# Cross attention taken by two pairs of heads a step, with part of the score copies on ScalarE

## The chip, the cores and the metric

The kernel runs on one core of one Trainium2 chip. A core has TensorE (PE, the matrix engine; PEld is its loading of the stationary operand), VectorE (DVE), ScalarE (ACT), GpSimd (POOL) and SyncE (SP), which here only issues transfers. Matrix products are written to PSUM, of which this kernel uses eight banks of 128x512 float32 values (two pools, of seven and of one), and read from there by VectorE or ScalarE; everything else on the chip lies in SBUF, and the DMA queues move data between SBUF and memory (HBM, "dram" tiles in the code). The metric is the device time of one execution in microseconds (us), lower is better, as the median of several runs. An error bound on the output has to be kept, and float32 products have to stay float32.

## The reference, cut to what matters

One block of a perceiver: eight batches (B) of 128 rows (S) with 512 features (D) attend to 2048 context rows (J) of 384 features, then to themselves, then pass a feed-forward layer. LayerNorm without parameters stands ahead of each of the three.

```python
def cross(x, context, Wq, Wk, Wv, Wo, bo):          # x is already normalized
    q = (x @ Wq).reshape(B, 128, 8, 64)              # 8 heads of 64
    k = (context @ Wk).reshape(B, 2048, 8, 64)
    v = (context @ Wv).reshape(B, 2048, 8, 64)
    sim = jnp.einsum('bihd,bjhd->bhij', q, k) * 64 ** -0.5
    attn = jax.nn.softmax(sim, axis=-1)
    out = jnp.einsum('bhij,bjhd->bihd', attn, v).reshape(B, 128, 512)
    return out @ Wo + bo

def self_attention(m, Wq, bq, Wk, bk, Wv, bv):       # m is normalized
    logits = (m @ Wq + bq) @ (m @ Wk + bk).T         # a batch at a time
    logits = where(causal, -inf, logits)
    probs = softmax(logits, axis=1) / sqrt(512)      # over the queries
    return m + probs @ (m @ Wv + bv)

def ffn(x, w1, b1, w2, b2):                          # h and w2 in an 8-bit float
    h = relu(x @ w1.T + b1)
    return fq16(fq8(h) @ fq8(w2).T + fq16(b2))

x = x + cross(layernorm(x), context, ...)
x = x + self_attention(layernorm(x), ...)
x = x + ffn(layernorm(x), ...)
```

## The kernel before

**Cross attention, batch by batch.** The main loop (L925 to L1005) goes over eight batches b and, in each, over four pairs of heads m. Of a pair, `scores` (L499) makes 128x2048 scores of each of two heads: for each of four stretches of 512 keys it fills two banks, one per head, by matmuls on 64 rows of the array each (a head has 64 features, so two heads stand above one another: tile 64*128 in the profile). VectorE moves each bank into the tile `p` and takes its maximum along the way (L515); L521 and L523 make the negated, scaled maximum `nm` of the pair from the eight partial ones. `exps` (L532) is one ScalarE instruction per head over 2048 keys, with the row sums as a by-product. `turns` (L540) turns `p` in 32x32 blocks by eight VectorE transposes, four per head (L548), and 16 DMAs issued by SyncE put the blocks into `pT` (L554), which has the keys on partitions. `attend` (L559) multiplies `pT` by v into the accumulating bank `po`; each head fills 64 columns of the array (tile 128*64).

`after_strips` (L526) is a one-element ScalarE copy that reads a partial maximum, set between a pair's scores and the transfers that ScalarE issues next.

**Keys and values as units.** K and V of a batch come out of four units: `k_proj` for each half of the heads (kt0, kt1) and `v_proj` for each half of the context rows (v0, v1). A unit is a `block_product` (L300): a fast matrix multiplication in which sums of blocks of the operands (`x_both` and `m_both`, made by GpSimd in `next_half`, L828; `wk_sums` and `wv_sums`) are multiplied in 20 products instead of more, and the results are combined while leaving PSUM. It uses seven banks, and into several of them later products are added after an earlier state has been read:

```python
mm(z3, 7, True)
mm(z3, 8, False)
take((2, 0), z3)
yield
mm(z1, 12, True)
mm(z2, 19, True)
take((1, 0), z2)
mm(z3, 2, False)
```

`take` is a ScalarE copy from a bank into the result (L328), `with_bank` and `less_bank` are VectorE additions and subtractions with a bank (L331, L334). The three `yield`s divide a unit into parts of 2, 5, 4 and 9 products; `first_of(unit)` writes the next part, `all_of(unit)` the rest. Later in the unit the fourth product on z4 follows `with_bank((3, 1), z4, add, (3, 1))`, and the second on z2 follows `take((1, 0), z2)`, as above. A K product is two matmuls of 512 columns (of 256 in the first batch's `k_proj(0, 1, (1,))`, which makes only half of the keys), a V product four of 256 columns.

In a step (b, m) the order is: scores of pair m, products with v of the pair before, first exponential, the unit's first part, second exponential, transposes and strips, the rest of the unit. The units of a batch make the keys and values of the next; in the first batch `k_proj(0, 1, (1,))` and `v_proj(0, 1)` stand in m = 0, and `both_weights` (L289) between them. `project` (L673) multiplies the result of a batch by wo (held in SBUF all along) in the first step of the next and adds it to the rows x; `norm_rows` (L650) and others then make the normalized, turned rows for self attention, spread over the steps m = 1 to 3, and ScalarE's queue writes them out.

**Ahead of and behind the loop.** `turn_weight` (L275) turns the two weights of self attention by VectorE transposes and 16 SyncE issues each (L284) into `turned_w`; `both_weights` multiplies the two with one another (tile `pw`, 32 matmuls) and writes the result to memory. Self attention (class `SelfAttention`, two groups sa0 and sa1 of four batches) fills steps of the last batch and follows it, then comes the feed-forward layer.

**What sets the order.** The order of TensorE, and of VectorE and ScalarE in the loop, is that of the program text (manual schedule, with lists in which ScalarE and VectorE work). SyncE's and GpSimd's instructions are ordered by the scheduler. An engine works through its list, and an instruction in it waits for the semaphores of what it depends on. Places in SBUF come from pools by tag: a new tile of a tag waits until the last reader of the tile that had the place before is done. Here `pp` (the tile `p`) and `ptp` (`pT`) have one place each, `qtp` two, `tmp` and `xp` two each, `wop` holds wq and later wo, and `keep` holds the weights of K and V at the start and later every second v0.

Of the kernel before, what the change touches and what calls it, by code (L numbers as in the profile page):

```python
# [25 lines left out]
def tile_perceiver_block(  # L26
# [35 lines left out]
    TMPB = 2  # L62
# [7 lines left out]


# [4 lines left out]
    keep = ctx.enter_context(tc.tile_pool(name="keep", bufs=1))  # L76
# [28 lines left out]
    ktp, vp, qtp, wop = right("ktp", 1), right("vp", 1), right("qtp", 2), right("wop", 1)  # L105
    pp, ptp, tmp, xp = right("pp", 1), right("ptp", 1), right("tmp", TMPB), right("xp", 2)
# [100 lines left out]
    w_in = keep.tile([P, 2, NKC, D], F32, tag="keep", name="w_in")  # L207
# [24 lines left out]
    wq = load_w(wop, xa_wq, NK, "wq", nc.sync)  # L232
# [27 lines left out]
    def spread_biases():  # L260
        for n in range(2):
            bias_rows.append(tmp.tile([P, D], F32, tag="t", name=f"row_{n}"))
            nc.gpsimd.dma_start(bias_rows[n], across(n))
# [11 lines left out]
    def turn_weight(i):  # L275

        if i == 0:
            turned_w.append(vp.tile([P, 2, NK * NK, P], F32, tag="v0", name="turned_w"))
        for k in range(NK):
            nc.vector.transpose(w_sa[:, i, k], w_sa[:, i, k])  # L280
        t = turned_w[0][:, i]
        w = w_sa[:, i].rearrange("p k (m g j) -> p g (k m) j", m=NK, g=Q)
        for a, g in STRIPS:
            nc.sync.dma_start(t[ts(g, SQ), :, ts(a, SQ)], w[ts(a, SQ), g])  # L284
# [4 lines left out]
    def both_weights():  # L289

        tq, tk = (turned_w[0][:, i].rearrange("p (k m) c -> p k m c", m=NK) for i in range(2))
        for n in range(NK):
# [5 lines left out]
            t = xp.tile([P, D], F32, tag="x", name=f"both_{n}")  # L298
            nc.scalar.copy(t, ps)
            nc.scalar.dma_start(both_w[:, n], t)  # L300
            if n == 1:
                yield
# [123 lines left out]
    def v_proj(b, h):  # L426


        pool, tag = (keep, "keep") if h == 0 and b % 2 == 0 else (vp, f"v{h}")
        v = pool.tile([P, 4, 2, D], F32, tag=tag, name=f"v_{b}_{h}")  # L430
# [65 lines left out]
    def scores(b, m):  # L496
# [8 lines left out]
        home, tag = (ktp, "kt0") if (b, m) == (B - 1, 2) else (pp, "p")  # L505
        p = home.tile([P, Q, 2, J // Q], F32, tag=tag, name=f"p_{b}_{m}")
        for n in range(NJ):
# [6 lines left out]
            for i in range(2):  # L514
                nc.vector.tensor_scalar(  # L515
                    p[:, :, i].rearrange("p g (t i) -> p t g i", i=SQ)[:, ts(n, Q)],
                    pair[i].rearrange("p (t g i) -> p t g i", g=Q, i=SQ),
                    1.0, None, ALU.mult, ALU.max, accum_out=mx[:, i, n : n + 1],
                )
# [4 lines left out]
        ps_[b, m], nms[b, m], mxs[b, m] = p, nm, mx  # L524

    def after_strips(b, m):  # L526


        seen = small.tile([P, 1], F32, tag="seen", name=f"seen_{b}_{m}")
        nc.scalar.copy(seen, mxs[b, m][:, 0, 0:1])  # L530
# [9 lines left out]
    def turns(b, m):  # L540

        p = ps_[b, m]
        pt = ptp.tile([P, Q, 2, J // Q], F32, tag="pT", name=f"pT_{b}_{m}")
        for i in range(2):
            for _, g in STRIPS[:Q]:
                nc.vector.transpose(p[:, g, i], p[:, g, i])  # L548
        turned_[b, m] = pt.rearrange("p a h (t i) -> p h t a i", i=SQ)

        def strips(engines, some):

            for i, (a, g) in enumerate(some):
                engines[i % len(engines)].dma_start(pt[ts(g, SQ), a], p[ts(a, SQ), g])  # L554

        return strips
# [34 lines left out]
    def spread_sums(b):  # L591
        line = wides[b]
        rs = wides[b] = tmp.tile([P, D], F32, tag="t", name=f"rs_{b}")
        for i in range(2):
# [3 lines left out]
            )  # L598

    def inverse_sums(b):  # L600
# [3 lines left out]
        wide = tmp.tile([P, NH, DH], F32, tag="t", name=f"wide_{b}")  # L604
        nc.vector.tensor_copy(wide, rden.unsqueeze(2).to_broadcast([P, NH, DH]))
        wides[b] = wide.rearrange("p h d -> p (h d)")

    def normalized_first(b):
# [4 lines left out]
        rs = tmp.tile([P, D], F32, tag="t", name=f"rs_{b}")  # L613
# [14 lines left out]
    def load_x(b):  # L628
        xs[b] = xp.tile([P, D], F32, tag="x", name=f"x_{b}")
        nc.scalar.dma_start(xs[b], xd[:, b, :])  # L630

    def load_u(b):
        u = tmp.tile([P, D], F32, tag="t", name=f"u_{b}")
        nc.scalar.dma_start(u, u_line)
        stats[b] = (u,)

    def row_stats(b):
# [4 lines left out]
        stats[b] += (mv,)  # L642

    def row_scale(b):
        sd = small.tile([P, 1], F32, tag="sd", name=f"sd_s_{b}", bufs=4)
        nc.scalar.activation(sd, stats[b][1][:, 1:2], AF.Sqrt, bias=eps)
# [4 lines left out]
    def norm_rows(b):  # L651

        u, mv, sd = stats[b]
        rs = small.tile([P, 1], F32, tag="rs", name=f"rs_s_{b}", bufs=4)
        nc.vector.reciprocal(rs, sd)
        xn = tmp.tile([P, D], F32, tag="t", name=f"xn_s_{b}")
        nc.vector.tensor_scalar(xn, xs[b], mv[:, 0:1], rs, ALU.subtract, ALU.mult)
        pt = bank(f"pt_s_{b}")
        row_constant(b, xn, u, pt)
        nc.vector.tensor_tensor(xs[b], xs[b], xn, ALU.add)  # L660
        for k in range(NK):
            nc.tensor.transpose(pt[:, ts(k, P)], xn[:, ts(k, P)], ident)
        xt = tmp.tile([P, NK, S], F32, tag="t", name=f"xt_s_{b}")
        nc.scalar.copy(xt, pt.rearrange("p (k t) -> p k t", k=NK))
        stats[b] = xt
# [7 lines left out]
    def project(b, ot):  # L673
        ps = bank(f"py_{b}")
        for k in range(NK):
            nc.tensor.matmul(  # L676
                ps, ot[:, ts(k, P)], wo[:, k, :], start=(k == 0), stop=(k == NK - 1)
            )
        nc.vector.tensor_tensor(xs[b], ps, xs[b], ALU.add)

    rows = {}

    def bring_last_rows():
        rows[0] = keep.tile([P, B, D], F32, tag="keep", name="rows")
        nc.gpsimd.dma_start(rows[0][:, B - 2 :], xd[:, B - 2 :])
        for r in range(B):
            xs[r] = rows[0][:, r, :]

    def bring_rows():
        nc.scalar.dma_start(rows[0][:, : B - 2], xr[:, : B - 2])  # L690

# [11 lines left out]
    class SelfAttention:  # L703


        def __init__(self, g, pool, w):
            self.g, self.pool = g, pool
            self.both, self.swv, self.bv, self.u, self.mask = w
            self.rows = [g * GB + i for i in range(GB)]
            self.xt = pool.tile([P, NK, GT], F32, tag=f"xt{g}", name=f"xt_{g}")  # L710
            there = slice(g * GT, min((g + 1) * GT, (B - 2) * S))
# [121 lines left out]
    def enter_self_attention():  # L833
        src.close()
        wsa = ctx.enter_context(tc.tile_pool(name="wsa", bufs=1, reuse_waits="tile"))
        sap = ctx.enter_context(tc.tile_pool(name="sap", bufs=1, reuse_waits="tile"))
        both = wsa.tile([P, NK, D], F32, tag="both", name="both")
        nc.gpsimd.dma_start(both, both_w)
        w = [both, wsa.tile([P, NK, D], F32, tag="swv", name="swv")]
        sa0 = SelfAttention(0, sap, w + [None] * 3)  # L840
        nc.gpsimd.dma_start(w[1], sa_wv.rearrange("(k p) n -> p k n", p=P))
        w += [load_row(wsa, sa_bv, "bv"), load_row(wsa, u_line, "u")]
# [7 lines left out]
        w.append(mask)  # L850
        sa0.bv, sa0.u, sa0.mask = w[2:]
        return sap, w, sa0
# [22 lines left out]
    bo = tmp.tile([P, D], F32, tag="t", name="bo")  # L875
# [12 lines left out]

    wo = load_w(wop, xa_wo, NK, "wo", nc.sync, tag="wq")

# [27 lines left out]
    def turned_rows(g, rows, tag):  # L918

        xt = sap.tile([P, NK, GT], F32, tag=tag, name=f"xf_{g}")  # L920
# [4 lines left out]
    sa0 = None  # L925
    for b in range(B):
        last = b + 1 == B
        for m in range(NK):
            scores(b, m)

            if m % 2 and not last:
                after_strips(b, m)
            if m == 0 and b > 0:
                after_strips(b, m)
                spread_sums(b - 1)
            if m == 1 and b > 0 and not last:
                load_u(b - 1)
            if m == 3 and b > 0 and not last:
                nc.scalar.dma_start(xtd[:, :, ts(b - 1, S)], stats[b - 1])
                nc.scalar.dma_start(xr[:, b - 1, :], xs[b - 1])  # L940
            if m == 3 and b < B - 2:
                load_x(b)
            unit = None
            if m > 0:
                attend(b, m - 1)
            elif b > 0:

                attend(b - 1, NK - 1)
# [329 lines left out]
```

## Time and profile before

| | |
|---|---|
| median of 3 runs | 1082.82 us (1082.68 to 1082.97) |
| profiled execution, span | 1080.4 us |
| TensorE busy | 1074.7 us, 99% |
| VectorE busy | 756.8 us, 70% |
| ScalarE busy | 350.6 us, 32% |
| GpSimd busy | 249.0 us, 23% |
| granted TensorE clock | full in all 40 slices |
| moved by DMA | 136.62 MB, 126 GB/s |
| read from HBM | 55.85 MB |

The span is the time from the first to the last instruction in the one execution that was profiled; the time of a run also holds what lies around it. Busy times overlap between engines. In the chain of work that ended last, each line is a start, a duration, an engine, a tile with a line of the program, and a number of instructions. Matmul ends are modelled in the profile, and a few of their records can be missing. The costliest groups of VectorE and ScalarE, with their count, sum and mean duration of one, and the idle time ahead of them with what ended it:

```profile
L548 DVE STREAM_TRANSPOSE p<-p 128x512 f32<-128x512 f32 x256 | 158.9, 679 | 62.2 <-ACT p L535 62.0
L535 ACT ACTIVATE p<-p,nm 128x2048 f32<-128x2048 f32 x64 | 128.2, 2004 | 210.7 <-DVE nm L523 103.3
L515 DVE TENSOR_SCALAR_CACHE_REDUCE p<-sc 128x512 f32<-128x512 f32 x256 | 159.0, 686 | 20.9 <-PE sc L511 20.9
...
L328 ACT COPY v<-pv_z 128x512 f32<-128x512 f32 x112 | 62.8, 585 | 55.3 <-PE pv_z L435 55.0
```

VectorE is idle for 62 us ahead of transposes, until exponentials end, and ScalarE for 103 us ahead of exponentials, until the maxima are there; TensorE is in neither wait.

### The profile page before, as it was taken

How to read it: one execution, taken by the hardware profiler on the slowest of the kernel's cores; microseconds unless marked ns; L12 is line 12 of the kernel's file. 1: busy time of each engine (PE TensorE's matmuls, PEld its weight loads, DVE VectorE, ACT ScalarE, POOL GpSimd, SP SyncE). 2: the span in 40 equal slices, each digit the busy share in tenths (PEclk: the TensorE clock that was granted, in tenths of full speed). 3: DMA queues.
4: the chain of work that ended last, by engine and by line, in shares of the span. 5: the costliest groups of instructions: out<-in, count | busy, mean ns of one | idle time of the engine just before them, and what ended most of it. 6: DMA issues, size and time to landing. Idle time of an engine off the chain costs nothing.

```text
span 1080.4 us, 15603 instructions
## 1 busy us (share of the span) xinstructions
PE 1074.7 (99%) x5614; PEld 706.4 (65%) x5614; DVE 756.8 (70%) x1639; ACT 350.6 (32%) x559; POOL 249.0 (23%) x379
## 2 busy tenths in 40 slices
PE   9999999999999999999999999999999999999998
PEld 5485774577467657755775577557746656768875
DVE  5876567778777877787688778777877657584333
ACT  3322133324332422433243324332433222323221
POOL 0154130360055005500540262036100312000000
PEclk9999999999999999999999999999999999999999
DMA  9476334553565456535544653455345744431001
GB/s 328 139 189 152 118 78 98 146 148 84 131 166 137 93 135 164 139 86 150 152 110 99 165 147 79 117 147 147 80 111 127 235 121 147 175 106 31 10 12 58
DMA packets 74013, 136.62 MB, mean 126 GB/s; under 512 B 29376, under 2 KB 37840, under 8 KB 72912
## 3 DMA queue, kind: packets, MB, share of 16 engines
q1 hardware_dynamic: 61264, 113.03, 40.8%
q10 hardware_dynamic: 8464, 11.54, 3.6%
q0 software_dynamic: 4208, 11.06, 3.3%
q8 instruction: 45, 0.74, 0.3%
q14 instruction: 32, 0.26, 0.1%
HBM read 55.85 MB, written 10.52 MB: 61 GB/s over the span
## 4 chain that ended last, share of the span: by engine, by line
PE 98%; SPq 1%; DVE 1%; issue 0%; ACT 0%; DMA 0%; POOL 0%; POOLq 0%
PE pv_z L435 21%; PE pk_z L412 20%; PE po L566 11%; PE sc L511 10%; PE pv_b L435 4%; PE pk_b L412 3%; PE ph_b L1104 3%; PE psk L749 3%; PE psv L793 3%; PE py L676 3%; PE pq L479 3%; PE pf L1152 2%; PE ph_c L1104 2%; PE ph_a L1104 2%; PE k L395 2%; PE ph L1056 1%
## 5 line engine op out<-in xcount | busy, mean ns | idle before, releaser
L548 DVE STREAM_TRANSPOSE p<-p 128x512 f32<-128x512 f32 x256 | 158.9, 679 | 62.2 <-ACT p L535 62.0
L535 ACT ACTIVATE p<-p,nm 128x2048 f32<-128x2048 f32 x64 | 128.2, 2004 | 210.7 <-DVE nm L523 103.3
L515 DVE TENSOR_SCALAR_CACHE_REDUCE p<-sc 128x512 f32<-128x512 f32 x256 | 159.0, 686 | 20.9 <-PE sc L511 20.9
L435 PE MATMUL pv_z<-wv_sums,x_both 128*128 128x256 f32 x640 | 157.9, 381 | 0.0
L412 PE MATMUL pk_z<-x_both,wk_sums 128*128 128x512 f32 (+1 forms) x320 | 149.2, 572 | 0.7 <-ACT kt L328 0.6
L435 PEld LDWEIGHTS pv_z<-wv_sums,x_both 128*128 128x128 f32 x640 | 120.4, 190 | 18.6 <-issue 2.5
L566 PEld LDWEIGHTS po<-pT,v 128*64 128x64 f32 x2048 | 111.1, 137 | 23.8 <-issue 23.1
L566 PE MATMUL po<-pT,v 128*64 128x128 f32 x2048 | 118.8, 274 | 0.0
L511 PE MATMUL sc<-kt,q 64*128 64x512 f32 x512 | 118.5, 602 | 0.0
L435 PE MATMUL pv_z<-wv_sums,m_both 128*128 128x256 f32 x448 | 107.3, 379 | 0.0
L412 PEld LDWEIGHTS pk_z<-x_both,wk_sums 128*128 128x128 f32 x320 | 59.2, 190 | 66.9 <-issue 55.0
L412 PE MATMUL pk_z<-m_both,wk_sums 128*128 128x512 f32 (+1 forms) x224 | 101.3, 568 | 0.0
L588 POOL DMA_DIRECT2D line_s<-inverse x28 | 14.5, 525 | 350.8 <-DVE inverse L585 350.8
L435 PEld LDWEIGHTS pv_z<-wv_sums,m_both 128*128 128x128 f32 x448 | 84.2, 190 | 12.6 <-POOL x_both L165 0.6
L165 POOL TENSOR_TENSOR m_both<-x_both 128x256 f32<-128x256 f32 x70 | 51.0, 729 | 175.3 <-DMA x_both<-in_ctx_t_dram 113.9
L511 PEld LDWEIGHTS sc<-kt,q 64*128 64x128 f32 x512 | 46.9, 186 | 65.6 <-issue 54.0
L328 ACT COPY v<-pv_z 128x512 f32<-128x512 f32 x112 | 62.8, 585 | 55.3 <-PE pv_z L435 55.0
L328 ACT COPY kt<-pk_z 128x512 f32<-128x512 f32 (+1 forms) x112 | 59.7, 562 | 58.3 <-PE pk_z L412 57.9
L530 ACT COPY seen<-mx 128x1 f32<-128x1 f32 x21 | 4.0, 191 | 209.2 <-DVE p L515 209.2
L412 PEld LDWEIGHTS pk_z<-m_both,wk_sums 128*128 128x128 f32 x224 | 40.8, 190 | 46.8 <-issue 35.1
L165 POOL TENSOR_TENSOR x_both<-x_both 128x256 f32<-128x256 f32 x98 | 69.9, 727 | 3.0 <-DMA x_both<-in_ctx_t_dram 2.7
L331 DVE TENSOR_TENSOR v<-pv_z,v 128x512 f32<-128x512 f32 x96 | 63.1, 685 | 5.5 <-PE pv_z L435 5.5
(212 smaller groups left out, 1312.8 us busy)
## 6 DMA issues: line engine op xcount, KB each, us to landing
pT<-p SPq DMA_DIRECT2D x488, 128.0 KB, 2.4
x_both<-in_ctx_t_dram SPq DMA_DIRECT2D x45, 512.0 KB, 5.2
w<-in_w_t_dram SPq DMA_DIRECT2D x1, 4096.0 KB, 13.9
w2f<-in_w_t_dram SPq DMA_DIRECT2D x16, 256.0 KB, 2.7
pT<-p POOLq DMA_DIRECT2D x24, 128.0 KB, 3.9
x_in<-in_x_dram SPq DMA_DIRECT2D x8, 256.0 KB, 6.4
qd<-xq SPq DMA_DIRECT2D x8, 256.0 KB, 2.5
q<-qd SPq DMA_DIRECT2D x8, 256.0 KB, 4.1
```

Source lines behind the costliest of these rows:

```text
L165: eng.tensor_tensor(x_block(b, h, to), x_block(b, h, one), x_block(b, h, two), ALU.add if op == "+" else ALU.subtract,)
L328: nc.scalar.copy(outs[ij], views(ps))
L331: nc.vector.tensor_tensor(outs[to], views(ps), outs[other], op)
L412: nc.tensor.matmul(ps[:, : n * BK], wk_sums[:, WSLOT[WAT[r]], f2, :], x_block(b, hs, XAT[r]), start=start, stop=True, skip_group_check=True,)
L435: nc.tensor.matmul(ps[:, ts(t, 256)], x[:, ts(t, P)], wv_sums[:, WSLOT[WAT[r]], :], start=start and t == 0, stop=True, skip_group_check=True,)
L479: nc.tensor.matmul(ps, wq[:, k, ts(m, P)], xt[:, k, :], start=(k == 0), stop=(k == NK - 1),)
L511: nc.tensor.matmul(pair[i], q[r, :], kts[b, m // 2][r, m % 2, ts(n, 512)], start=True, stop=True)
L515: nc.vector.tensor_scalar(p[:, :, i].rearrange("p g (t i) -> p t g i", i=SQ)[:, ts(n, Q)], pair[i].rearrange("p (t g i) -> p t g i", g=Q, ...
L535: nc.scalar.activation(p[:, :, i], p[:, :, i], AF.Exp, bias=nms[b, m][:, i : i + 1], scale=SCALE, accum_out=sums[b][:, h : h + 1],)
L548: nc.vector.transpose(p[:, g, i], p[:, g, i])
L566: nc.tensor.matmul(pos[b][h * DH : (h + 1) * DH, ts(m, P)].rearrange("p (a i) -> p a i", a=Q), v[:, jt % 8, ts(2 * m + h, DH)], turned_[b, ...
L1104: nc.tensor.matmul(self.ps[to][:, ts(t, HR)], w[:, q, 2 * self.d + t], x[:, q], start=start and t == q == 0, stop=True, skip_group_check=True,
```

## The change

A step now takes two pairs of heads, "one" and "two": `scores` of both (sixteen banks), then `attend` of both pairs of the step before, then two units. So the loop has two halves per batch: in half 0 the two `v_proj` of the same batch (in the first batch `k_proj(0, 1, (1,))` and `v_proj(0, 1)`), in half 1 the two `k_proj` of the next batch. Three of the eight banks of each pair are copied into `p` by ScalarE, and VectorE takes their maxima from `p` afterwards, in the new function `maxima`:

```diff
+    COPIED = ((1, 0), (2, 1), (3, 0))
...
             for i in range(2):
-                nc.vector.tensor_scalar(
-                    p[:, :, i].rearrange("p g (t i) -> p t g i", i=SQ)[:, ts(n, Q)],
-                    pair[i].rearrange("p (t g i) -> p t g i", g=Q, i=SQ),
-                    1.0, None, ALU.mult, ALU.max, accum_out=mx[:, i, n : n + 1],
-                )
+                to = p[:, :, i].rearrange("p g (t i) -> p t g i", i=SQ)[:, ts(n, Q)]
+                of = pair[i].rearrange("p (t g i) -> p t g i", g=Q, i=SQ)
+                if (n, i) in COPIED:
+                    nc.scalar.copy(to, of)
+                else:
+                    nc.vector.tensor_scalar(
+                        to, of, 1.0, None, ALU.mult, ALU.max, accum_out=mx[:, i, n : n + 1]
+                    )
+        ps_[b, m], mxs[b, m] = p, mx
+
+    def maxima(b, m):
+
+        p, mx = ps_[b, m], mxs[b, m]
+        for n, i in COPIED:
+            nc.vector.tensor_reduce(
+                mx[:, i, n : n + 1], p[:, :, i, ts(n, P)], axis=AX.XY, op=ALU.max
+            )
```

`after_strips` is gone, `turns` takes one head at a time, and `strips` is a function of its own. The loop:

```diff
     for b in range(B):
         last = b + 1 == B
-        for m in range(NK):
-            scores(b, m)
...
+        for half in range(2):
+            one, two = 2 * half, 2 * half + 1
+            scores(b, one)
+            scores(b, two)
+            if half == 0 and b > 0:
+                bring_home(b - 1)
+            if half == 1 and not last:
+                load_q(b + 1)
...
+            before = (b, 0) if half else (b - 1, 2)
+            if before[0] >= 0:
+                attend(before[0], before[1])
+                attend(before[0], before[1] + 1)
+            maxima(b, one)
+            maxima(b, two)
...
+            exps(b, one, 0)
+            exps(b, one, 1)
+            turns(b, one, 0)
+            if half == 0 and b > 0:
+                ot = normalized(b - 1, wides[b - 1])
+            turns(b, one, 1)
+            strips(b, one, [nc.sync])
+            first_of(unit)
+            exps(b, two, 0)
...
+            first_of(unit)
+            turns(b, two, 0)
+            exps(b, two, 1)
+            if half == 0 and b > 0:
+                project(b - 1, ot)
+            first_of(unit)
+            turns(b, two, 1)
+            strips(b, two, [nc.sync])
+            if half == 0 and b > 0:
+                row_stats(b - 1)
+                row_scale(b - 1)
+            if half == 1:
+                sums_along_rows(b)
+            all_of(unit)
+            unit = units[1]
+            if half == 0 and b > 0:
+                norm_rows(b - 1)
+                next_half(b + 1, 0)
+                first_of(unit)
+                first_of(unit)
+                turn_rows(b - 1)
+            all_of(unit)
+            if half == 0:
+                next_half(b + 1, 1)
```

Places: `pp` and `ptp` now have two places each, `qtp` one, every v0 lies in `vp`, and `keep`, `tmp`, `xp` and `wop` are gone. What lay there at the start (w_in, wq, bias rows, `turned_w`, the copies of `pw`) lies in the places of `p` and `pT`. wo and the rows that the projection and the normalization need lie in the place of the first keys, kt0, once the scores that read those keys are done; wo (1 MB) is loaded anew for every batch, by SyncE, and three rows tiles by ScalarE's queue:

```diff
+    def bring_home(b):
+
+        home = homes[b] = ktp.tile([P, 2 * NK, D], F32, tag="kt0", name=f"home_{b}")
+        nc.sync.dma_start(home[:, :NK], xa_wo.rearrange("(k p) n -> p k n", p=P))
+        line, rs = wides[b], home[:, NK]
...
+        wides[b] = rs
+        xs[b] = home[:, NK + 1]
+        nc.scalar.dma_start(xs[b], xd[:, b, :])
+        nc.scalar.dma_start(home[:, NK + 2], u_line)
```

`norm_rows` no longer turns the rows: the sum of x and the normalized rows goes to GpSimd, and `turn_rows`, inside the second V unit, does the transposes and writes both out. `both_weights` moves from inside the first step to ahead of the first scores:

```diff
     turn_weight(1)
     all_of(values)
     next_half(1, 0)
-
-    wo = load_w(wop, xa_wo, NK, "wo", nc.sync, tag="wq")
-
+    both_weights()
```

Behind the loop the order changes. In half 1 of the last batch the first unit is the keys of sa0 (`sa0.keys`) and there is no second; the batch's logits, exponentials, two batches' values and probabilities of sa0 come ahead of the last two `attend`, which stood among them before; batch 7's rows alone (before: 6 and 7) are normalized from memory at the end; and the value weights of self attention are loaded a second time, beside w1, for the values made after the place is given up. The number of matmuls is the same.

## The prediction

> **What bounds the kernel now.** I read the page first: busy times, granted clock, shares of the chain that ended last.
>
> ```profile
> span 1080.4 us, 15603 instructions
> ...
> PE 1074.7 (99%) x5614; PEld 706.4 (65%) x5614; DVE 756.8 (70%) x1639; ACT 350.6 (32%) x559; POOL 249.0 (23%) x379
> ...
> PEclk9999999999999999999999999999999999999999
> ...
> PE 98%; SPq 1%; DVE 1%; issue 0%; ACT 0%; DMA 0%; POOL 0%; POOLq 0%
> ```
>
> TensorE is busy for all but 5.7 us, at full clock, and is 98% of the chain. So the change can only gain inside TensorE's own stream, and it loses wherever it makes TensorE wait. Next, the chain of waits for one step of an inner batch, and for one unit that follows no attention step:
>
> ```profile
> 535.69 3.43 PE py L676 x8
> 539.12 3.63 PE sc L511 x16
> 542.75 3.64 PE po L566 x64
> 546.40 6.26 PE pv_z L435 x28
> ```
> ```profile
> 66.53 6.04 PE pv_z L435 x28
> ```
>
> Scores (64x128 tiles), products with v (128x64) and projection (128x128) each stream eight times 512 columns. The projection, whose shape is its neighbours', takes 3.43; scores and products 0.20 and 0.21 more. The unit's first 28 matmuls cost 6.26 after products with v and 6.04 after another unit: 0.22. So each passage to another tile shape costs about 0.2 us. From a scores start (436.37) to the next batch's (539.12) is 102.75 us.
>
> Then the timelines of ScalarE and VectorE in one step, which give the pitch of each link that TensorE will wait for:
>
> ```profile
> 573.60 2.01 ACT L535 ACTIVATE p<-p,nm 128x2048 f32<-128x2048 f32 x1
> 575.50 0.19 ACT L535 ACTIVATION_READ_ACCUMULATOR p<-p,nm 128x1 f32 x1
> 575.59 0.57 ACT L664 COPY xt_s<-pt_s 128x512 f32<-128x512 f32 x1
> 576.06 1.57 ACT L328 COPY kt<-pk_z 128x512 f32<-128x512 f32 x3
> ```
> ```profile
> 575.72 2.49 DVE L548 STREAM_TRANSPOSE p<-p 128x512 f32<-128x512 f32 x4 [0.67 <-ACT p L535]
> 578.14 0.65 DVE L334 TENSOR_TENSOR kt<-kt,pk_z 128x512 f32<-128x512 f32 x1
> 578.79 0.69 DVE L331 TENSOR_TENSOR kt<-pk_b,kt 128x512 f32<-128x512 f32 x1
> ```
>
> Start to start: one exponential 2.0, one copy out of a bank 0.5, four transposes 2.4, one addition 0.6. In the same view eight score evacuations go every 0.61 and the negated maximum is ready 0.5 after the last.
>
> **The change, part by part.** Durations are of this execution, 1080.4 us; the median of the runs is 1082.8, so 2.4 is added at the end.
>
> *Fewer passages.* 32 groups of scores, 32 of products and as many returns to units become 16 of each. 48 passages less at 0.2 (0.18 to 0.21): **-9.3** (-8.7 to -10.1). As a check, a batch is four times 7.27 of scores and products, 80 products of units at 0.858 or 0.863, 3.43 of projection, 0.44 of transposes, four returns at 0.2: 102.6 of 102.75, so little else is there to win. The number of matmuls stays.
>
> The Trainium skill ("TensorEngine Tiling (Array Packing)", Key Properties) says that changing the tiling mode drains TensorE, which agrees with the 0.2 us. "TensorE: Matmul & The Clock Gate", Single matmul latency, gives a warm constant of 398 cycles at 2.4 GHz; taken for one drain that is an estimate of 0.166 us, and this part would be -8.0 instead.
>
> *Evacuating 16 banks.* From the scores' start (t=0) TensorE needs 2x3.43+0.2 = 7.06. VectorE's ten evacuations need 6.1, ScalarE's six copies 3.0 to 3.6: both keep up and end near 7.7. New are six maxima by VectorE over what ScalarE copied. No row is like them: between 0.16 (the small reduction over maxima) and 1.2 (twice an evacuation); I take 0.6, the row of their size. Exponentials of the first pair then run 10.2 to 14.2.
>
> *Second half of a batch (seven times).* Products with v end at 14.13 and two K units follow. By the unit's text a product accumulates into a bank that is still being read, so it waits for the reader. ScalarE's list: copy (2,0) at 16.09 (two products at 0.86), the second pair's first exponential to 18.57, four copies. VectorE: the subtraction from (0,1) at 19.7, behind the second of these; four transposes of the second pair to 22.7; bank b4's subtraction to 23.3; four more transposes to 25.7; reciprocal and small transpose for the sums 0.35; the subtraction from (2,0) and the addition to (3,1) end at 27.45. The fifteenth product (z4 again) needs that last one, at 14.33+14x0.858 = 26.35. It waits 1.15 us: 7 x 1.15 = **+8.0** (0 if VectorE is 1.1 sooner; 7x2.5 = 17.5 if exponentials and copies don't overlap as assumed).
>
> *First half (seven times).* The projection between unit parts gives VectorE 3.43 more; the same addition ends at 29.9, needed at 29.85: **+0.7** (0 to 4).
>
> *First step of all.* Here nothing to be multiplied with v stands between scores and units: the half-size unit k(0,1) starts at 7.26 and its products take 0.43. Its fifth accumulates into z3 and needs copy (2,0), which is listed behind both exponentials of the first pair: 14.6 instead of 9.0. The seventh needs copy (1,0), behind the next exponential: 16.97. The thirteenth needs (3,1), behind four copies and the last exponential: 20.3. The fifteenth needs VectorE's addition to (3,1), behind four transposes: 23.6; then six products of 0.43, end 26.15 instead of 15.86: **+10.3** (8.7 if the maxima cost 0.16; 12 if 1.2). The same unit before took 10.25, 87.36 to 97.61, for 8.8 of work, waiting for one exponential:
>
> ```profile
> 93.37 0.70 PE L412 MATMUL pk_z<-x_both,wk_sums 128*128 128x256 f32 x2 [0.56 <-ACT kt L328]
> ```
>
> That goes: **-1.45**. Before, two parts of the unit were listed ahead of that one exponential.
>
> The Trainium skill ("PSUM — Partial Sum Buffer", Engine vs sequencer instructions) calls ScalarE's and VectorE's queues strict FIFO, and so speaks against this order. By it a copy waits out the exponential ahead of it, as in the row above; were it to overtake, this part would be about 0.
>
> *Weights for self attention.* Their products (pw, 13.7 us of TensorE) move ahead of the first scores, to 83.8, and need the turned weights from 32 issues of SyncE:
>
> ```profile
> L284 SPq DMA_DIRECT2D turned_w<-w_sa x32: 585/632/1914, 63.8 to 89.3; - x32
> ...
> DMA to landing us min/median/max: 2.1/2.3/6.4
> ```
>
> They were needed at 97.4 and hid behind scores and the k unit; now nothing hides the end. Their tile no longer shares a place with the first q rows, so the first sixteen can begin earlier. The second sixteen wait for VectorE's transposes of the second weight, which start to end at 72.37 and 74.85; then 15 x 0.672 + 2.3 gives 87.3: **+3.5** (up to 7.7 with the issues where they were; 2.5 if the first matmuls need only early strips).
>
> *Moved at no cost.* SyncE loads 1 MB of wo per batch into the keys' place; needed at 20.4, and by x_both's 5.2 us for 0.5 MB lands near 13 (uncovered: a few us per batch). ScalarE's queue brings sums and rows by 13.2, needed 14.7. SyncE's 32 strips per step end inside it (16 issues take 9.5 to 11.8) and are multiplied one step later; x_both's sums on POOL (20 at 0.69) are done near 18, needed 24.6.
>
> *Tail.* The last batch's logits now wait for their keys (0.7), and VectorE's conversion of feed-forward weights stands ahead of some values: **+1.0**. Bounds: before has 5.7-1.45 of other idle, of which at most 3 could go; +5 if all eight groups of conversions are in the way.
>
> **Sum:** -9.3 +8.0 +0.7 +10.3 -1.45 +3.5 +1.0 = +12.75; 1080.4 + 12.75 + 2.4 = **1095.6 us**.
>
> **Rivals.** (1) *No wait in the second halves*: VectorE's last addition comes by 26.35. For it: 1.1 us is two VectorE instructions in a list of some 25. Against: none of the listed durations is long. 1095.6 - 8.7 = 1086.9. (2) *Faster: VectorE's list ends early everywhere.* With maxima at 0.16 and transposes that follow the exponentials at once, the seven waits go, and in the first step the thirteenth product's wait (20.3 less 1.6) becomes the last: with eight products of 0.43 it ends at 22.1, so 10.3 becomes 6.3. -10.1 +6.3 -1.45 +2.5 = -2.75, with the tail at nothing: 1080.1. It decides once the new waits together are under 10.1 + 1.45 - 2.2 = 9.4 us; here they are 8.8. Against: eight evacuations at 0.61 and four transposes at 2.4 are steady over the whole trace, and copies behind exponentials are ScalarE's, not VectorE's. (3) *Both halves wait longer*: maxima at 1.2 put VectorE 3.6 later per half, past the slack of the exponentials (2 us): 14 halves at 1.6 more are less than 22, say two thirds of it: 1095.6 + 14 = 1110. (4) *It does not do what it says*: the 0.2 is not the passage but the first wait of a group; then 9.3 stays unsaved, 1104.9. The projection without it speaks against.
>
> **Chances.** Forecast 0.48, rival 1 0.20 (0.06 of it inside 0.2%), rival 2 0.20 (0.15 clearly faster, 0.05 inside), rivals 3 and 4 0.12. A measurement tells 0.2% (2.2 us) from no change. Faster 0.15, same 0.11, slower 0.74. The range 1080 to 1109 leaves out some 0.12 of rival 2 and 0.06 of rivals 3 and 4; the forecast's own is 1089 to 1103.
>
> **What would show it.** Scores in groups of 32 matmuls of 7.06 us, products of 128; batches of about 102.6, with idle before the fifteenth product put down to VectorE's L331 in K units only; in the first k unit three idles put down to ScalarE's L328, some 10 us; idle of 3.5 ahead of pw; the maxima at 0.6. Wrong if the batch falls to 100.5 (the second half hides all) or if the first unit runs in under 13 us.

## The result and the profile after

The changed kernel takes 1167.46 us (median of 4 runs, 1161.34 to 1183.91) against 1082.89 of the kernel before: a ratio of 1.0764, with a 95% interval of 1.0732 to 1.0796; the ratio leaves out the slowest of the four runs, which lies more than 1.5% above the fastest. The direction was forecast, the size was not: 1095.6 us had been predicted, and the range ended at 1109.

First the page of the profiled execution after (span, busy times, granted clock by slices, chain):

```profile
span 1168.1 us, 15597 instructions
...
PE 1096.1 (94%) x5614; PEld 719.9 (62%) x5614; DVE 799.8 (68%) x1537; ACT 407.3 (35%) x637; POOL 251.8 (22%) x370
...
PEclk9998899999999799989998999899899999999999
...
PE 74%; DVE 11%; POOL 5%; DMA 4%; ACT 2%; issue 1%; SPq 1%; ACTq 0%; DVEq 0%; POOLq 0%
```

TensorE's share of the chain has fallen from 98% to 74%. It is idle for 72 us instead of 5.7, and the same 5614 matmuls are busy for 21 us longer, with the granted clock below full in several slices. So two things happened: waits, and slow running after them. Where? The windows below go from one start of scores to the next, for the first batch's second half and the halves of batches 1 to 3 (columns: window, its length, busy time and instructions of each engine, granted clock, share of DMA, GB/s):

```profile
core 0: us, PE busy (x) PEld busy (x) DVE busy (x) ACT busy (x) POOL busy (x), PEclk, DMA share, GB/s
...
149.30:199.40 50.10, 49.22 (x243) 25.08 (x242) 37.81 (x74) 19.48 (x28) 15.87 (x24) 1.00 0.49 117
199.40:252.50 53.10, 53.10 (x334) 42.13 (x334) 41.61 (x81) 23.04 (x33) 1.71 (x1) 1.00 0.53 131
252.50:309.20 56.70, 50.92 (x243) 25.64 (x242) 37.90 (x74) 19.48 (x28) 29.57 (x44) 0.97 0.49 128
309.20:362.40 53.20, 53.20 (x335) 42.23 (x334) 41.66 (x81) 23.04 (x33) 1.71 (x1) 1.00 0.55 130
362.40:428.30 65.90, 54.35 (x242) 26.90 (x242) 55.88 (x74) 19.58 (x28) 29.53 (x44) 0.90 0.43 112
428.30:481.40 53.10, 53.10 (x334) 42.13 (x334) 41.54 (x81) 23.04 (x33) 1.71 (x1) 1.00 0.54 130
481.40:546.30 64.90, 52.66 (x243) 26.32 (x242) 54.84 (x74) 19.58 (x28) 29.47 (x44) 0.92 0.42 113
```

First halves take 53.0 to 53.2 us, and TensorE is busy throughout. The second half of the very first batch takes 50.1. The second halves of the later batches take 56.7, 65.9, 64.9, 57.5, 58.9 and 57.1: 60.4 us more than six times 50.1. POOL's column says what differs: its sums of context rows (29.5 us, both halves of `x_both`) fall into these windows as a whole, and in the first halves it has 1.7 us of work; in the first batch's second half it is 15.9. The kernel before did them in two portions per batch, 20 sums (13.8 us) in one step and 20 in the next (three of its steps, columns as above):

```profile
511.00:536.00 25.00, 25.00 (x162) 20.31 (x163) 19.44 (x41) 8.08 (x12) 13.86 (x20) 1.00 0.57 146
536.00:561.00 25.00, 25.00 (x156) 18.86 (x155) 17.49 (x39) 11.14 (x16) 13.84 (x20) 1.00 0.57 147
561.00:588.00 27.00, 27.00 (x136) 14.76 (x135) 22.36 (x48) 8.37 (x12) 0.00 (x0) 1.00 0.43 94
```

Why do both sets of sums come at once? The chain of waits in the first half of batch 1, up to the first sum (ACTq and SPq are the issuing of a transfer by ScalarE and SyncE, DMA is the time until it has landed):

```profile
242.03 0.60 ACTq L668
...
242.67 2.71 DMA xr<-home
...
245.39 0.51 SPq L556
...
249.82 0.51 SPq L126
...
250.37 5.32 DMA x_both<-in_ctx_t_dram
...
255.83 0.73 POOL m_both L165
```

ScalarE issues the writes of the normalized rows (`turn_rows`, L668 and L669) in the middle of the second V unit. A strip of the second pair (L556, SyncE) starts when such a write has landed. The strip shares no data with the write; but in the built list of instructions it carries a wait for it: as the program built from the kernel assigns them, transfers of SyncE and ScalarE count their completions on the same eight semaphores in turn, and a transfer waits for the one before it on its semaphore. Of the second pair's sixteen strips the ninth and the tenth wait for the two writes in this way, and the six behind them wait with them. Behind the strips stand SyncE's loads of both halves of the next batch's context rows (L126), six issues one after another:

```profile
673.82 33.65 SPq L556 DMA_DIRECT2D pT<-p  x32
707.58 3.71 SPq L126 DMA_DIRECT2D x_both<-in_ctx_t_dram  x6
```

In batch 5 (this timeline of SyncE's queue) the place of the first half was free at about 692, when the first V unit ended; the loads were issued at 707.6, 2.5 us before the second half began. What that leads to in two second halves: TensorE's timeline of the changed kernel in batch 5 (start, length, line, operation, and in brackets the idle time before and what ended it):

```profile
730.76 3.78 PE L412 MATMUL pk_z<-x_both,wk_sums 128*128 128x512 f32 x4 [6.35 <-POOL x_both L165]
734.34 3.59 PE L412 MATMUL pk_z<-m_both,wk_sums 128*128 128x512 f32 x6
```

and VectorE's timeline of the same kernel in batch 2:

```profile
374.73 0.16 DVE L531 TENSOR_REDUCE top<-mx 128x2 f32<-128x8 f32 x1
374.93 18.51 DVE L533 TENSOR_SCALAR nm<-top 128x2 f32<-128x2 f32 x1
```

The K unit's first product waits 6.35 us for GpSimd's sums, and the first four matmuls then take 3.78 us where 1.9 is usual: the granted clock from 730.7 to 738 is 0.63. And in batches 2 and 3 the negated maximum of the second pair, an instruction on 128x2 numbers with a median of 0.17 us, takes 18.5 and 17.8. All 32 of the changed kernel, and under them those of the kernel before (behind the count the least, median and largest duration in ns, then when the first and last began):

```profile
L533 DVE TENSOR_SCALAR nm<-top x32: 169/170/18512, 115.4 to 946.3; 128x2 f32<-128x2 f32 x32
```
```profile
L523 DVE TENSOR_SCALAR nm<-top x32: 168/170/752, 90.1 to 896.2; 128x2 f32<-128x2 f32 x32
```

GpSimd works without a gap meanwhile, instruction after instruction at 0.69 us, and its last sum ends at 393.4, the moment at which the maximum ends:

```profile
392.69 0.72 POOL L165 TENSOR_TENSOR x_both<-x_both 128x256 f32<-128x256 f32 x1
```

The exponentials, ScalarE's copies and so TensorE's second wait of this half (5.64 us) hang on it.

### The profile page after: what moved, and what is told of

Read it like the earlier page. It is cut to its first block, busy times and chain, and to the rows that moved or that the text cites. A ratio compares the mean times of both kernels' runs of the same rounds, so it can differ in the third digit from the quotient of the medians.

```text
span 1168.1 us, 15597 instructions
## 1 busy us (share of the span) xinstructions
PE 1096.1 (94%) x5614; PEld 719.9 (62%) x5614; DVE 799.8 (68%) x1537; ACT 407.3 (35%) x637; POOL 251.8 (22%) x370
## 4 chain that ended last, share of the span: by engine, by line
PE 74%; DVE 11%; POOL 5%; DMA 4%; ACT 2%; issue 1%; SPq 1%; ACTq 0%; DVEq 0%; POOLq 0%
PE pv_z L434 18%; PE pk_z L412 15%; PE sc L509 7%; PE po L566 6%; DVE nm L533 3%; PE ph_b L1091 3%; PE pv_b L434 3%; DVE p L548 3%; POOL x_both L165 3%; PE pk_b L412 2%; PE pq L478 2%; PE py L680 2%; PE pf L1139 2%; POOL m_both L165 2%; DMA x_both<-in_ctx_t_dram 2%; PE ph_c L1091 2%
## 5 line engine op out<-in xcount | busy, mean ns | idle before, releaser
L412 PE MATMUL pk_z<-x_both,wk_sums 128*128 128x512 f32 (+1 forms) x320 | 159.2, 610 | 32.9 <-POOL x_both L165 32.9
L412 PE MATMUL pk_z<-m_both,wk_sums 128*128 128x512 f32 (+1 forms) x224 | 108.3, 595 | 24.6 <-ACT kt L328 18.0
L412 PEld LDWEIGHTS pk_z<-x_both,wk_sums 128*128 128x128 f32 x320 | 63.8, 203 | 105.3 <-issue 54.2
L518 DVE TENSOR_SCALAR_CACHE_REDUCE p<-sc 128x512 f32<-128x512 f32 x160 | 102.8, 688 | 33.4 <-PE sc L509 29.4
L516 ACT COPY p<-sc 128x512 f32<-128x512 f32 x96 | 56.1, 586 | 173.5 <-PE sc L509 172.3
L566 PE MATMUL po<-pT,v 128*64 128x128 f32 x2048 | 115.3, 273 | 0.0
L659 POOL TENSOR_TENSOR home<-home 128x512 f32<-128x512 f32 x7 | 11.9, 1707 | 409.4 <-DVE home L658 409.4
L412 PEld LDWEIGHTS pk_z<-m_both,wk_sums 128*128 128x128 f32 x224 | 44.0, 203 | 82.2 <-issue 50.7
L509 PEld LDWEIGHTS sc<-kt,q 64*128 64x128 f32 x512 | 49.9, 187 | 62.3 <-issue 47.3
L334 DVE TENSOR_TENSOR kt<-kt,pk_z 128x512 f32<-128x512 f32 (+1 forms) x48 | 29.7, 647 | 69.4 <-ACT kt L328 69.4
```

The lines of the kernel that those rows point to most:

```text
L412: nc.tensor.matmul(ps[:, : n * BK], wk_sums[:, WSLOT[WAT[r]], f2, :], x_block(b, hs, XAT[r]), start=start, stop=True, skip_group_check=True,)
L509: nc.tensor.matmul(pair[i], q[r, :], kts[b, m // 2][r, m % 2, ts(n, 512)], start=True, stop=True)
L516: nc.scalar.copy(to, of)
L518: nc.vector.tensor_scalar(to, of, 1.0, None, ALU.mult, ALU.max, accum_out=mx[:, i, n : n + 1])
L566: nc.tensor.matmul(pos[b][h * DH : (h + 1) * DH, ts(m, P)].rearrange("p (a i) -> p a i", a=Q), v[:, jt % 8, ts(2 * m + h, DH)], turned_[b, ...
```

## The experiments

All are compared with the kernel before in the same session (1082.5 to 1082.9). The theories are called Q (SyncE's queue is held by the rows' writes), P (VectorE's maximum waits for GpSimd's port) and V (the prediction's: VectorE's and ScalarE's own lists).

**Rows written later.**

```diff
         nc.scalar.copy(xn, pt)
+
+    def write_rows(b):
+
+        xn = homes[b][:, NK + 3]
         nc.scalar.dma_start(xtd[:, :, ts(b, S)], xn.rearrange("p (k t) -> p k t", k=NK))
         nc.scalar.dma_start(xr[:, b, :], xs[b])
...
             if half == 1 and not last:
+                if b > 0:
+                    write_rows(b - 1)
                 load_q(b + 1)
...
                 turn_rows(b - 1)
+                if last:
+                    write_rows(b - 1)
```

> The two writes of normalized rows that ScalarE issues in the middle of the second V unit are issued in the second half instead, behind its scores. Theory Q (queue): in the first half of batches 1 to 6 the last eight strips of the second pair wait for these writes (SyncE stands from about +33 to +45 of the half), SyncE's loads of the next context rows stand behind the strips, both halves' loads and GpSimd's 40 sums come at once, and the K unit waits for the sums. Then the second halves of batches 1 to 6 (56.7, 65.9, 64.9, 57.5, 58.9, 57.1 us) fall to batch 0's 50.1, about -60 in all: some 1107 us. Theory V (the prediction's): these halves wait for VectorE's and ScalarE's own lists; then nothing changes, 1167 us. Theory P (port) by itself: the 18 us maxima of batches 2 and 3 stay, about 16 us of the loss with them.

Measured: 1136.8 us (1125.6 to 1148.6). The first halves stay at 53.2. Of the six second halves two fall to 50.05; four stand at 57.4 to 58.3, with VectorE's maximum waiting up to 9.4 us in them. TensorE waits for GpSimd's sums nowhere any more (before the edit 32.9 us). So Q is right about the sums and V is wrong; but Q's 1107 was not reached, because the sums still run while the maxima are due.

**The maximum by the accumulating form.**

```diff
-        nc.vector.tensor_scalar(nm, top, -SCALE, None, ALU.mult)
+        nc.vector.tensor_scalar(nm, top, -SCALE, None, ALU.mult, ALU.max, accum_out=unread)
```

> The changed kernel, with the negated maximum (128x2, VectorE) written by the form of the operation that also accumulates. Theory P (port): the plain form waits until GpSimd pauses, which took 18.5 and 17.8 us in the second halves of batches 2 and 3; the other form does not wait. Then these two halves fall from 65.9 and 64.9 to the 57 to 59 of the others: -14 to -16, some 1151 us, and no such instruction is over 0.3 us. If the long instruction is a sign of something else (late scores, a slow semaphore), nothing changes: 1167 us. Theory Q's 6 us of waiting for GpSimd's sums per batch stay in both cases.

Measured: 1152.2 us (1151.2 to 1155.4), as P has it. All 32 maxima take the same time (this kernel's line, read as above):

```profile
L534 DVE TENSOR_SCALAR_CACHE_REDUCE nm<-top x32: 154/155/156, 115.3 to 929.8; 128x2 f32<-128x2 f32 x32
```

The waits for the sums stay, 26.3 us.

**Both edits.**

> Both edits. By Q the sums no longer run in one stretch behind the scores, so P has little left to act on: within 3 us of the run with the later rows alone, about 1107 us. If P also acts on the batches' shorter waits (0.3 to 0.8 us instead of 0.17), 1 to 3 us less than that.

Measured: 1105.4 us (1103.6 to 1105.9), ratio 1.0208 (1.0191 to 1.0225). The two edits act on one another: the first alone brought 31 us, the second alone 15, together 62 (the changed kernel's own runs scatter, so these differences are good to some 3 us). The profiles say the same: the six second halves are 60.4 us over 50.1 each in the changed kernel, 31 over with the rows later alone, 44 with the accumulating form alone, and nothing with both. 31 and 44 are more than 60.4: each cause also holds up part of what the other holds up. The windows of two second halves with both edits, columns as above:

```profile
250.60:300.70 50.10, 49.22 (x243) 25.08 (x242) 37.25 (x76) 19.50 (x28) 19.05 (x29) 1.00 0.51 130
...
353.90:403.90 50.00, 49.12 (x242) 24.98 (x242) 37.25 (x76) 19.50 (x28) 20.67 (x32) 1.00 0.51 129
```

and SyncE's timeline in the first half between them:

```profile
317.43 21.78 SPq L557 DMA_DIRECT2D pT<-p  x32
339.32 14.97 SPq L126 DMA_DIRECT2D x_both<-in_ctx_t_dram  x6
```

32 strips are issued in 21.8 us instead of 33.7, the loads begin 38.7 us after the half's scores instead of 50.7, and the second halves take what the first batch's took. TensorE is busy for 1076.4 us instead of 1096.1: 19.7 of the loss were matmuls at a lower clock after waits.

**First step.** The half-size K unit of the first step whole, ahead of the exponentials (`all_of(unit); unit = units[1]` in front of `exps(b, one, 0)` when b and half are 0).

> Both edits, and in the very first step the half-size K unit is written out whole before the first exponentials, which then go with the V unit as in every other half. The prediction puts 10.3 us on that unit's copies standing behind exponentials: the unit then takes 8.6 to 9 us instead of about 19, and 1 to 2 us come back in the V unit: 8 to 9 us less than the run with both edits, some 1098 us. If the unit waits for its banks or for the sums of the context rows instead, less than 3 us.

Measured: 1102.8 us (1100.4 to 1103.1). The unit takes 10.3 us instead of 19.4, not far from the 8.6 to 9 expected, but only 2.6 us come out: the first batch is shorter by 5.0 (scores of its second half now wait 2.2 us for a bank that ScalarE copies, and the copy waits 4.4 for this step's strips), product pw starts 0.9 later, and 1.9 are lost in the tail, which the edit doesn't touch: from the last scores to the end it takes 235.4 us instead of 233.5. Apart from the last one below, every other changed run has 234.9 to 236.3 there, so it is the profile with both edits that is short, and why stays open.

**Transposes behind the unit's work.** In the second halves `turns(b, two, 1)` and its strips move behind `all_of(unit)`.

> On top of the run with both edits (1105.4): in the second halves the transposes of the second pair's second head, with their strips, stand behind the first K unit's VectorE work instead of in the middle of it. The prediction has the fifteenth product wait 1.15 us for them in each of seven halves; the run with both edits shows 8 waits of 8.0 us in all on VectorE in K units. If those transposes are what it waits for: second halves fall from 50.05 to about 49.1, some -6, 1099 us. If it is the earlier four transposes or ScalarE's copies, less than 2 us. If the later strips come too late for the next products with v: slower.

Measured: 1099.1 us (1096.4 to 1101.1); second halves take 48.89 instead of 50.05 us, 1.16 less, and TensorE doesn't wait in them. Seven times 1.16 is 8.1; 6.3 come out, since the tail is 1.9 longer here too. The strips are not too late.

**The start in the order of before.** The step (0, 0) written out: scores of the first pair, K unit with an exponential inside, `both_weights()`, scores of the second pair, V unit.

> On top of the run with both edits (1105.4): the first step is put back to the order of before (scores of the first pair, half-size K unit with one exponential inside, product of the two weights, then scores of the second pair, V unit). The prediction puts 10.3 us on the first unit and 3.5 on the product of the weights; the profile of the changed kernel shows 89 instead of 84 for the latter's start and 3 us of slow clock in it. Expected: first batch's second half starts about 14 us sooner, 1091 us. If the cost of the start lies elsewhere (loads, turned weights late in any order): less than 5 us.

Measured: 1096.7 us (1096.6 to 1097.2), 8.7 less, 5 short of what was expected. The second half of the first batch starts 10.4 us sooner (137.05 instead of 147.41). pw no longer waits and runs at full clock; but the K unit still waits 2.5 us for a copy that stands behind the exponential, which waits for maxima that VectorE does behind the unit's subtraction.

**Start and transposes together.**

> Both of the above on top of the run with both edits. If the terms of the sum are independent places, the gains add: 1105.4 - 6 - 14, some 1085 us; that is 2 us above the kernel before, and what is left is the tail (about 5 us) against the saved passages (about 7).

Measured: 1088.2 us (1087.3 to 1090.1), 17.2 less than with both first edits alone. Alone they brought 8.7 and 6.3, which makes 15.0: the two places add, and 2 us come on top. Most of these are the tail again: it is about 1.4 to 1.9 longer in each of the two runs, and so is counted twice in their sum, but once here.

**No copies by ScalarE.** `COPIED = ()`, on top of both edits.

> On top of the run with both edits: no bank is copied by ScalarE; VectorE evacuates all sixteen with the maximum along the way, and the six separate maxima are gone. The prediction holds that the division between the two engines is not on the path. VectorE does 16 x 0.61 = 9.8 us instead of 6.1 + 3.7, ScalarE 3 us less per half, the second pair's scores wait for banks up to 0.5 us: within 5 us of 1105. If the copies are what lets TensorE run through the scores (16 banks in 7.1 us against 9.8 us of VectorE): scores of 9.5 instead of 7.2 us, +35 us.

Measured: 1169.0 us (1168.0 to 1170.9), outside both expectations, and not by the evacuation: scores take 7.86 instead of 7.19 us. ScalarE's queue and SyncE's show why. The row's write in ScalarE's timeline of this kernel, ahead of a second half:

```profile
584.40 0.57 ACTq L673 DMA_DIRECT2D xtd<-home  x1
```

and the loads of context rows in SyncE's:

```profile
590.89 3.38 SPq L126 DMA_DIRECT2D x_both<-in_ctx_t_dram  x6
```

The scores of this second half start at 592.0. With no copy of scores ahead of them in ScalarE's list, the rows' writes went out 7.6 us before that, strips waited for them again, and TensorE waited 40.2 us for GpSimd's sums. The copies had been what held the writes back, as the next run shows.

**No copies, writes held.** A one-element ScalarE copy from the second pair's maxima ahead of the writes, as `after_strips` did in the kernel before.

> The run without ScalarE's copies again (1169), with a one-element ScalarE copy from the second pair's maxima ahead of the writes of the rows. In the run without it ScalarE reached these writes 7 us before the second half began, since no copy of scores stood ahead of them; SyncE's loads again came behind the last strips, 3 us before the half's scores ended, and K units waited 40 us for GpSimd's sums. Theory Q: the hold brings the second halves back to about 50.7 and the whole to 1115 us, 10 above the run with the copies (scores take 7.9 instead of 7.2 us in 15 halves). If VectorE's sixteen evacuations themselves are what costs 64 us: about 1169.

Measured: 1117.2 us (1115.6 to 1119.4); second halves 50.7. So one instruction of some 0.2 us decides over 52 us by where it lets two transfers begin, and the copies themselves are worth 11.8 us (1117.2 less 1105.4), most of it in the scores (7.86 against 7.19 us, 16 times). That is more than the 5 us expected of them, so the division of the banks does lie on the path, by 0.67 us per half.

**Best of these.** On top of start and transposes: `maxima(0, 0)` ahead of the K unit's first part, and the reads of the last two batches of self attention behind `hidden(0, xfs[0], range(1, 4))`.

> On top of the run with start and turns (1088.2): in the first step the maxima of the first pair stand ahead of VectorE's unit work (its unit waits 2.5 us for a copy behind the exponential that waits for them), and the last two products of probabilities and values of self attention go behind the feed-forward's next three blocks (TensorE waits 2.5 us for VectorE there and then runs some 2 us at a lower clock). If these are the two places, -2 and -4: some 1082 us, level with the kernel before. If VectorE's conversions are late for anything that comes behind as well: 1086 to 1090.

Measured: 1081.36 us (1080.81 to 1082.20, 11 runs) against 1082.77, a ratio of 0.9988 (0.9979 to 0.9997): 1.4 us less, under the 2.2 us that the prediction took for the least difference that can be told from none. Its page:

```profile
span 1078.9 us, 15660 instructions
...
PE 1070.5 (99%) x5614; PEld 710.7 (66%) x5614; DVE 762.6 (71%) x1569; ACT 406.9 (38%) x637; POOL 255.3 (24%) x370
...
PEclk9999999999999999999999999999999999999999
```

TensorE's busy time is 4.2 us under the 1074.7 of the kernel before: the saved passages are there, once next to nothing waits.

## Why the prediction was wrong, step by step

| step of the sum | predicted | measured in the profile after |
|---|---|---|
| fewer passages | -9.3 | -5.6: a batch without own waits takes 48.89 + 53.16 = 102.05 (run with the transposes moved) instead of 102.75, so 0.70 less, 8 times |
| second halves, own waits | +8.0 | +8.1: 1.16 per half, by the run that moves the transposes |
| first halves | +0.7 | about 0: TensorE doesn't wait in the 53.16 they take; counted above |
| first k unit | +10.3 | +10.8: 19.4 us, from 112.6 to 131.9, for 8.6 of work |
| stall of before | -1.45 | -1.45 |
| product of the weights | +3.5 | +8.0: 1.6 late by loads at the start, 3.5 of wait, 2.9 of slow clock |
| tail | +1.0 | about +7, an estimate, since the last batch's work is placed differently |
| context rows ("moved at no cost") | 0 | +60.4, with VectorE's waits for the port and the slow clock behind the waits |

The measured column adds up to +87.3, of a difference of spans of 87.7 (1168.1 less 1080.4); 0.4 are not assigned.

**The step that failed** is one sentence of "moved at no cost": "x_both's sums on POOL (20 at 0.69) are done near 18, needed 24.6". It reckoned with 20 sums, those of the second half of the context rows, and took for granted that the first half's had been loaded and summed before. Its pitch was right (0.69), the number was 40: in the six second halves they begin 1 to 2 us after the scores and end 30 to 32 us after them. For the loads stand in SyncE's queue behind 32 strips, and the prediction looked at when each transfer's place is free, and at how long strips take to issue (9.5 to 11.8 us for 16), but not at what a strip waits for besides its data: 32 took 33.7 us, and 21.8 once the writes were out of their way. The removal of `after_strips` stands among the changes and was cost at nothing. That instruction stood ahead of ScalarE's writes in the kernel before, and there they go out at 590.9 us, when the last strips before them have been issued by 586.6. That it was what kept them there was not tested in that kernel; the run with the writes held shows what such an instruction is worth in the changed one (1169.0 against 1117.2 us).

**The port** is the second part of the same term, and was not in the sum or among the rivals. The prediction has "the negated maximum is ready 0.5 after the last" evacuation, and left GpSimd's work out of it; with the rows later alone, where no product waits for sums, it still cost 31 us. The rows of before gave a hint that was not taken up: L523 there has a largest duration of 0.75 us beside a median of 0.17. The Trainium skill ("SBUF — State Buffer", Who interferes with whom) names tensor_scalar, save the form that also writes out its accumulator, among the VectorE instructions that can contend with GpSimd for a pair of ports that the two share. The runs agree on both halves of that sentence: up to 18.5 us in the one form, 0.155 in the other. It costs time only since GpSimd's sums came to lie where the maxima are due.

**The clock.** No term of the sum had TensorE run slower after a wait. In the changed kernel the granted clock is 0.63 from 730.7 to 738 after 6.35 us of idleness, and 0.50 in the first 4 us of pw after 3.5 us; with both edits, where most of the waits are gone, TensorE is busy for 19.7 us less. Waits of 0.7 to 2.2 us left no trace in the clock in any of the profiles. The Trainium skill ("TensorE: Matmul & The Clock Gate", Part 1) puts the fall to half clock after an idle window of about 3.4 us. That fits the two places, but the runs put the limit lower: after 2.51 us of waiting in the K unit (start in the order of before) the clock is 0.60 over the next 3 us, after 2.54 us in the tail (start and transposes together) 0.71, while after 2.52 and 2.60 us in other places (start and transposes together, both edits) it stays at 1.00. From 2.5 us on it can happen, and a wait of that length does not always bring it: even one of 3.50 us (ahead of pw, in the run with the writes held) did not.

**The passages** were the other term that was mis-sized. Doubling a group shows what its passage costs (from the group's start to the next start, two groups of before against one of after): scores save 2x3.63 - 7.19 = 0.07 us, products 2x3.64 - 7.14 = 0.14. The rest of the 0.2 grows with the group, so it is not the passage, as the fourth rival had it in part; the comparison with the projection's 3.43 misled. And 48 passages at 0.2 are 9.6, not 9.3.

**What held.** The timetable of the steps was good where the transfers were as assumed: the first batch's second half took 50.1 us (49.8 by the terms of the forecast), first halves 53.16 (53.05). The unit of the first step took 19.4 (18.9), and its last wait ended 23.7 us after the scores' start (forecast 23.6); but only 7.5 us of it are waits, two for ScalarE and one for VectorE, and 3.3 are matmuls at a low clock after the first wait of 5.5 (8.6 would be their time at full clock), which filled time that the forecast had as waiting. Where both defects are taken away the kernel takes 1105.4 us, 10 over the forecast: 3.7 are the passages, 2.6 the start (its first scores at 103.6, forecast 101.0), and some 3.6 the tail; the first halves' 0.7 did not come, and about 0.6 is not assigned.

Of the rivals, none named the mechanism. The third ("both halves wait longer", 1110) was nearest in size, but by VectorE's maxima, which took the 0.6 us that the forecast took.

## What to carry to other kernels

When a change moves work between steps, walk each queue that only issues transfers once more, and ask of every entry what it can be held by, completions of other queues' transfers included; a small instruction with no use for the data may be there to hold a transfer back, and its removal is priced by what it held. Then add up the engine that fills a gap (here GpSimd) over the whole window in which it must fit, not over the half that looks new. A wait of TensorE of 2.5 us or more could cost more than its length here, and an operation of VectorE on two numbers per partition took, in one form, as long as what was left of GpSimd's list.

## What the runs showed of the hardware that was not expected

- VectorE's 128x2 tensor_scalar was not let in between two GpSimd instructions: it waited through 27 of them in a row, 18.5 us, until the last sum of GpSimd's list was done. GpSimd's own instructions did not slow down (0.73 us each, as without the conflict).
- After a wait of 6.35 us four matmuls took 3.78 us instead of 1.9, at a granted clock of 0.63 over 7.3 us; second halves with waits of about 1 us have clock 1.00. Waits of 2.51 and 2.54 us were followed by a low clock, others of 2.52 and 2.60 were not.
- The kernel with the long waits spreads widely, 1161 to 1184 us and 1126 to 1149 with the rows later, where the others spread by at most 0.4%. These two are the changed kernels with the plain form of the maximum; probably they spread since whether a maximum meets a gap in GpSimd's sums is decided anew in each run, which was not shown.
